# Flamingo block on one core: preparing the first feed-forward's blocks in program order, with the bias part by part and the weight combining later

## The chip, the core and the metric

The kernel runs on one core of one Trainium2 chip. The metric is the device time of one execution in microseconds (us). Before the change three runs took 2104.38, 2107.78 and 2108.16 us; the median, 2107.78 us, is the time to compare with. One more execution was profiled: it took 2106.83 us, and its trace spans 2104.7 us from the first instruction to the last.

## What is computed

Eight sequences of 512 tokens with 512 features pass through two layers, each an attention and a feed-forward, all in float32, each behind a layer norm and added back through a gate. Cut to what matters:

```python
x = x + tanh(g_xattn[0]) * linear_cross_attention(layernorm(x), ctx)
x = x + tanh(g_ffn[0])   * (gelu(layernorm(x) @ proj1.T + b1) @ proj2.T + b2)    # 512 -> 2048 -> 512
x = x + tanh(g_xattn[1]) * masked_cross_attention(layernorm(x), ctx)
x = x + tanh(g_ffn[1])   * routed_experts(layernorm(x))                          # 8 groups, silu(gate) * up, down
```

The change is in the second of these lines, the *first feed-forward* (`ff0` in the code). The weights of the fourth line (`ff1`) are combined while `ff0` runs, and the change moves that work too.

## The kernel before

**Stages.** Sequence by sequence ("block" b = 0 to 7) the kernel does the first attention (`xa0`), then all eight blocks of `ff0`, then for each block the second attention with the second feed-forward (`ff1`). Between the stages x is kept in DRAM (`between`, line 137).

**Products by fewer multiplications.** Every large matrix product is done on 2 x 2 blocks with seven products in place of eight (a Strassen-like scheme). The seven are numbered 1 to 7; some operands are sums and differences that VectorE (DVE) makes first. In `ff0` a block has four *up units* (i = 0 to 3, class `Ff0Up`, line 838) and one *down* (512 outputs). An up unit does its products in the order 1, 2, 6, 5, 7, 4, 3 (`ORDER`, line 740), of which the last two are held back until the next unit has begun (`steps`, line 1192). Its products give four quarters a11, a12, a21, a22 of the activations (`part`, line 839: DVE adds, ScalarE (ACT) applies the gelu), and `combine_inner` (line 825: three DVE instructions) makes s1 = a21 + a22, s2 = s1 - a11 and a21 = a11 - a21 of them. It is called after part (1, 2), which product 3, the last of the unit, completes.

**The split down.** From block `ONCE` = 2 on the down is a `SplitDown` (line 928): each of its seven products is again done by seven inner ones, 56 matmul instructions in a product. Its order is `SPLIT_ORDER["ff0"]` = (1, 4, 2, 6, 5, 7, 3) (line 283), the last again held back into the next block. Product 1 reads a11, 4 reads a22, 2 reads a12, 6 reads s2. For each product `combine` (line 962) makes four sums on DVE (lines 969 to 972) in tiles named `split` (seven buffers); `at_once` (line 1009) copies the result out of the PSUM accumulator (ACT, lines 1011 and 1012) and queues eight DVE instructions that join the seven inner results and add them into x (lines 998 to 1007). The accumulator has five banks, handed out in turn (`acc_bank`, line 114). So the passage from the up units to the down, here called the *handover*, reads in TensorE's (PE) order: ... products 2, 6, 5, 7 of up unit 3, down 1, up 4 and 3 of unit 3, down 4, down 2, down 6, ...

**Preparing the next block** is a generator, `prep_ff0(b)` (line 576), advanced by the main loop (lines 1485 to 1497) at evenly spaced steps of the block before, `steps_of` (line 1436) = 5 times. `normed` (line 426) takes the statistics of the four 128-token parts (DVE, lines 435 to 440), the reciprocal root on GpSimd (POOL, line 442), and then, part by part, normalizes (`norm`, line 451, DVE) and turns (`turn`, line 458 PE, 461 ACT copy). For b > 0 the statistics and the first part come in one step. After the fourth part, `prep_ff0` adds the gated bias to all four parts at once (line 581, POOL), and at the end makes the four sums S (lines 570 to 573).

**The building of weights.** For each set of weights POOL makes three or four combinations (`combining`, line 233, lines 236 to 242); for a stream used by a split down four larger ones follow (lines 412 to 419). `build_weights` and `build_stream` (lines 355, 392) load raw weights (SyncE's queue, SP), yield once, combine in two calls, and store the results by DMA. They share one buffer (`build`, line 1420). The stream of `ff0` is built during blocks 0 and 1 (every second up step), the weights of `ff1` after that, one call for every third up step (line 1477): six sets for the up units, then three for the down.

**What sets the order.** A scheduler places the instructions of an engine; only an engine named in the set `in_order` keeps the program's order (class `Ordered`, line 47). In the feed-forward stages only SP's queue is kept (line 1414). SP also carries all weight loads, into a ring of 16 tiles (`RING`, line 130), each waiting until PE has done with the tile 16 places before. So the place of another DMA in SP's order sets when it is issued.

Of the kernel before, what the change touches and what calls it, by code (L numbers as in the profile page):

```python
# [33 lines left out]
NT = S // P  # L34
# [34 lines left out]
def flamingo_kernel(  # L69
# [23 lines left out]
    in_order = {"tensor", "vector", "scalar", "gpsimd", "sync"}  # L93
# [15 lines left out]
    def psum(name):  # L109
        return bank["ps"].tile([P, 512], F32, tag="ps", name=name)  # L110
# [25 lines left out]
    xs = {}  # L136
# [96 lines left out]
    def combining(eng, w):  # L233

        sub = ALU.subtract
        eng.tensor_tensor(w[5], w[3], w[1], sub)
        yield
        eng.tensor_tensor(w[1], w[1], w[0], sub)
        yield
        eng.tensor_tensor(w[4], w[3], w[1], sub)  # L240
        yield
        eng.tensor_tensor(w[6], w[2], w[4], sub)
        yield
# [36 lines left out]

    SPLIT_ORDER = {"ff0": (1, 4, 2, 6, 5, 7, 3), "ff1": (2, 4, 1, 6, 5, 7, 3)}
    SPLIT_CHUNKS = {"ff0": NF // 4, "ff1": NJ // 4}
    SPLIT_INNER = (1, 2, 4, 5, 6, 7, 3)
    SPLIT_SLOT = {1: 0, 6: 1, 2: 2, 3: 3, 4: 4, 5: 5, 7: 6}
# [68 lines left out]
    def build_weights(ph, tile7):  # L355

        todo = {
            "ff0": (("up", raw_p1, 4), ("down", raw_p2, 4)),
            "ff1": (("up", raw_gu, 6),),
        }[ph]  # L360
        todo = [(kind, raw, i) for kind, raw, n in todo for i in range(n)]

        def load(kind, raw, i):
            t = tile7(f"{ph}_{kind}{i}")
            raw(t, i)
            return t

        if ph == "ff1":
            for kind, raw, i in todo:
                t = load(kind, raw, i)  # L370
                yield
                yield from in_twos(combining(nc.gpsimd, t))
                for q in range(7):
                    nc.sync.dma_start(out=store[ph, kind, i, q], in_=t[q])
                yield
            return
        t = load(*todo[0])
        yield
        for n, (kind, raw, i) in enumerate(todo):
            following = load(*todo[n + 1]) if n + 1 < len(todo) else None  # L380
            yield from combining(nc.gpsimd, t)
            for q in range(7):
                nc.sync.dma_start(out=store[ph, kind, i, q], in_=t[q])
            yield
            t = following

    def in_twos(steps):
        for n, _ in enumerate(steps):
            if n % 2:
                yield  # L390

    def build_stream(ph, raw, tile7):

        place = [SPLIT_ORDER[ph].index(m) for m in (1, 5, 2, 3, 6, 7, 4)]
        for i in range(SPLIT_CHUNKS[ph]):
            t = tile7(f"{ph}_down{i}")
            w = [t[:, k] for k in place]
            raw(w, i)
            yield
            yield from in_twos(combining(nc.gpsimd, w))  # L400

            b = t.rearrange("p k n (h q) -> p k n h q", q=P)
            b11, b12, b21, b22 = (b[:, :, n, h] for n in range(2) for h in range(2))

            def keep(m, w):
                nc.sync.dma_start(out=stream[ph][:, :, SPLIT_INNER.index(m), i, :], in_=w)

            sub = ALU.subtract
            for m, w in ((1, b11), (2, b21), (3, b22)):
                keep(m, w)  # L410
            yield
            nc.gpsimd.tensor_tensor(b12, b12, b11, sub)
            keep(5, b12)
            yield
            nc.gpsimd.tensor_tensor(b22, b22, b12, sub)
            keep(6, b22)
            yield
            nc.gpsimd.tensor_tensor(b21, b21, b22, sub)
            nc.gpsimd.tensor_tensor(b11, b22, b11, sub)
            keep(4, b21)  # L420
            keep(7, b11)
            yield
        streamed.add(ph)


    def normed(ph, b, tag):

        xb = xs[ph, b]
        xnT = work.tile([P, NC, S], F32, tag="xnT", name=f"xnT_{tag}")
        mv = small.tile([P, NT, 2], F32, tag="mv", name=f"mv_{tag}")  # L430
        if ph == "xa0":
            in_order.add("vector")
        for t in range(NT):
            st = small.tile([P, 6], F32, tag="st", name=f"st_{tag}_{t}")
            nc.vector.bn_stats(st, xb[:, t, :])
            nc.vector.bn_aggr(mv[:, t, :], st)
        if b:
            in_order.discard("vector")
        var = small.tile([P, NT], F32, tag="var", name=f"var_{tag}")
        nc.vector.tensor_scalar(var, mv[:, :, 1], LN_EPS, None, ALU.add)  # L440
        rstd = small.tile([P, NT], F32, tag="rstd", name=f"rstd_{tag}")
        nc.gpsimd.tensor_tensor(rstd, var, neg_half, ALU.pow)
        if ph == "xa0" or tag.startswith("ff1") or tag == "ff0_0":
            yield
        if tag.startswith("ff1"):
            yield
        xn = {}

        def norm(t):
            xn[t] = work.tile([P, D], F32, tag="xn", name=f"xn_{tag}_{t}")  # L450
            nc.vector.tensor_scalar(  # L451
                xn[t], xb[:, t, :], mv[:, t, 0:1], rstd[:, t : t + 1], ALU.subtract, ALU.mult
            )

        def turn(t):
            pt = psum(f"pt_{tag}_{t}").rearrange("p (c q) -> p c q", q=P)
            for c in range(NC):
                nc.tensor.transpose(pt[:, c, :], xn[t][:, ts(c, P)], ident)  # L458

            at = t % 2 * 2 + t // 2 if tag.startswith("ff1") else t  # L460
            nc.scalar.copy(xnT[:, :, ts(at, P)], pt)

        if ph == "xa0" and b == 0:
            norm(0)
            norm(1)
            yield
            for t in range(NT):
                turn(t)
                if t + 2 < NT:
                    norm(t + 2)  # L470
                yield
            return xnT
        for t in range(NT):
            norm(t)
            turn(t)
            yield
        return xnT

# [86 lines left out]
    def token_combinations(ph, b, xnT):  # L565

        s = work.tile([P, 4, 2, H2], F32, tag="S", name=f"S_{ph}_{b}", bufs=1)
        a11, a12 = xnT[:, 0:2, 0:H2], xnT[:, 2:4, 0:H2]
        a21, a22 = xnT[:, 0:2, H2:S], xnT[:, 2:4, H2:S]
        nc.vector.tensor_tensor(s[:, 0], a21, a22, ALU.add)  # L570
        nc.vector.tensor_tensor(s[:, 1], s[:, 0], a11, ALU.subtract)
        nc.vector.tensor_tensor(s[:, 2], a11, a21, ALU.subtract)
        nc.vector.tensor_tensor(s[:, 3], a12, s[:, 1], ALU.subtract)
        return s

    def prep_ff0(b):
        xnT = yield from normed("ff0", b, f"ff0_{b}")

        xb = xs["ff0", b]
        for t in range(NT):  # L580
            nc.gpsimd.tensor_tensor(xb[:, t, :], xb[:, t, :], b2_sb, ALU.add)  # L581
        yield "last"
        blocks["ff0", b] = xnT, token_combinations("ff0", b, xnT)

# [183 lines left out]
    class Up(Unit):  # L768
# [50 lines left out]
        def rest(self, part):  # L819
            for _ in part:  # L820
                pass
# [12 lines left out]
    def open_inner(ph, b, n):  # L834
        for k in INNER:
            inner[k] = hpool.tile([P, n, H2], F32, tag=k, name=f"{k}_{ph}_{b}")

    class Ff0Up(Up):
        def part(self, r, c, p, s):
            if (r, c) == (1, 1) and self.i == 0:  # L840
                open_inner("ff0", self.b, NF // 2)
            h = inner[f"a{r}{c}"][:, ts(self.i, 2), :]
            if s is not None:
                nc.vector.tensor_tensor(h, p, s, ALU.add)  # L844
                p = h
            yield
            for n in range(2):
                f = NF // 2 * (c - 1) + 2 * self.i + n
                nc.scalar.activation(h[:, n, :], p[:, n, :], AF.Gelu, bias=b1_sb[:, f : f + 1])  # L849
            if (r, c) == (1, 2):  # L850
                combine_inner(ts(self.i, 2))


# [74 lines left out]
    class SplitDown(Unit):  # L928
# [9 lines left out]
        def __init__(self, ph, b):  # L938
            self.ph, self.b, self.tag, self.banks = ph, b, f"{ph}_{b}_down", {}
            self.chunks, self.order = SPLIT_CHUNKS[ph], SPLIT_ORDER[ph]  # L940
            self.combined, self.numbers = {}, {}
# [132 lines left out]
    class QUp(Up):  # L1074
        ph, i = "xa0", 0
# [195 lines left out]
    ticks = iter(range(10**6))  # L1271
# [162 lines left out]
    ticks = 0  # L1434

    def steps_of(ph, b, _):

        return 5 if ph == "ff0" else 24

    at, held = None, False  # L1440
    for u, m, n in plan:
# [30 lines left out]
        if u.kind == "up":  # L1472
            ticks += 1
            if "ff0" not in streamed:
                if ticks % 2 == 0:
                    next(again, None)
            elif ticks % 3 == 0:
                next(builder, None)
        if n + 1 == 3 * B:
            continue  # L1480
# [64 lines left out]
```

## Time and profile before

| what | us |
|---|---|
| median of three runs | 2107.78 |
| profiled execution, its own time | 2106.83 |
| its span, first to last instruction | 2104.7 |
| PE busy in the span | 2061.6 (98%) |
| DVE busy | 1451.9 (69%) |
| ACT busy | 596.6 (28%) |
| POOL busy | 318.0 (15%) |

How to read it: the page gives for each engine the time in which it had an instruction under way. A matmul's record lasts longer than its pitch (one of 128 x 256 is recorded at 380 ns, and a product of eight such takes 1.73 us in the chain of work), so PE counts as busy while it merely keeps up, and only gaps larger than that show as idle. The views used below are the busy time of each engine in chosen stretches, the waits, the timeline of an engine, and the chain of work that ended last. In PE's timeline product 1 of the split down starts at 644.75 us in block 2, and at 1135.64 us in block 7, the last block of `ff0`.

### The profile page before, as it was taken

Reading aid. Unit: us, or ns where it says so; the run is one execution under the profiler, and the core shown is the slowest. Engines: PE = TensorE matmul, PEld = TensorE weight load, DVE = VectorE, ACT = ScalarE, POOL = GpSimd, SP = SyncE. Lnnn points to the kernel's source line nnn. Section 1 sums busy time; section 2 is a strip of 40 time slices with the busy share of each in tenths; the row PEclk is TensorE's granted clock in tenths of the full one; section 3 lists DMA queues with packets and bytes.
Section 4 is the critical chain, followed back from the end, with each engine's and each line's share of the span. In section 5 each row is a group of like instructions: output and inputs, shape, how many; then the busy total and the mean of one; then the engine's idle time right before and its main releaser. Section 6 shows DMA issues by size and latency. Waiting matters only on the chain.

```text
span 2104.7 us, 34195 instructions
## 1 busy us (share of the span) xinstructions
PE 2061.6 (98%) x12460; PEld 1816.1 (86%) x12460; DVE 1451.9 (69%) x2727; ACT 596.6 (28%) x1236; POOL 318.0 (15%) x260
## 2 busy tenths in 40 slices
PE   8999999999999999999999999999999999999998
PEld 4778887788889998889898989898989889898988
DVE  3688777652528494868667777777777677876768
ACT  3433333222222324132334232213222222222121
POOL 3122111342413112240301010000000010100000
PEclk9999999999999999999999999999999999999999
DMA  7345633696869898888875858686776858585865
GB/s 227 120 155 155 209 132 93 214 306 220 294 220 330 285 307 288 283 298 281 297 248 190 304 163 276 198 264 214 229 237 189 283 170 293 157 284 161 269 204 169
DMA packets 306501, 485.12 MB, mean 230 GB/s; under 512 B 37024, under 2 KB 107840, under 8 KB 302240
## 3 DMA queue, kind: packets, MB, share of 16 engines
q1 hardware_dynamic: 298896, 456.18, 67.7%
q10 hardware_dynamic: 5856, 23.20, 2.9%
q0 software_dynamic: 1584, 3.57, 0.7%
q8 instruction: 100, 1.64, 0.3%
q14 instruction: 65, 0.53, 0.1%
HBM read 406.22 MB, written 76.61 MB: 229 GB/s over the span
## 4 chain that ended last, share of the span: by engine, by line
PE 74%; issue 10%; DVE 7%; DMA 4%; POOL 3%; SPq 1%; ACT 1%; ACTq 0%; POOLq 0%; DVEq 0%
PE x_ff L789 23%; PE w_ff L789 11%; PE x_ff_down L984 9%; PE w_ff_down L984 7%; PE z_ff L789 6%; PE z_ff_down L984 3%; PE v_ff_down L984 3%; PE x_ff_down L905 2%; SPq L60 1%; PE w_ff_down L905 1%; PE pt_ff L458 1%; PE pt_xa L458 1%; PE pst L609 1%; PE pr L654 1%; PE z_ff_down L905 1%
## 5 line engine op out<-in xcount | busy, mean ns | idle before, releaser
L789 PE MATMUL x_ff<-S_ff,w_ff_up 128*128 128x256 f32 x1280 | 304.5, 381 | 1.7 <-ACT u_ff L801 1.7
L789 PE MATMUL w_ff<-S_ff,w_ff_up 128*128 128x256 f32 x1280 | 303.6, 380 | 1.5 <-DVE a_ff L844 1.5
L789 PE MATMUL x_ff<-xnT_ff,w_ff_up 128*128 128x256 f32 x1280 | 294.1, 380 | 0.9 <-ACT u_ff L801 0.9
L801 ACT COPY u_ff<-x_ff 128x512 f32<-128x512 f32 x240 | 139.5, 582 | 539.2 <-PE x_ff L789 520.3
L789 PEld LDWEIGHTS x_ff<-S_ff,w_ff_up 128*128 128x128 f32 x1280 | 239.9, 190 | 42.6 <-issue 6.5
L789 PEld LDWEIGHTS w_ff<-S_ff,w_ff_up 128*128 128x128 f32 x1280 | 239.0, 190 | 34.2 <-DVE a_ff L844 2.3
L789 PEld LDWEIGHTS x_ff<-xnT_ff,w_ff_up 128*128 128x128 f32 x1280 | 238.4, 190 | 32.9 <-ACT u_ff L801 1.8
L789 PE MATMUL z_ff<-xnT_ff,w_ff_up 128*128 128x256 f32 x640 | 151.6, 379 | 0.0
L984 PE MATMUL x_ff_down<-w_ff_down,split_ff_down 128*128 128x128 f32 x1152 | 136.4, 275 | 2.8 <-DVE split_ff_down L972 1.9
L984 PEld LDWEIGHTS x_ff_down<-w_ff_down,split_ff_down 128*128 128x128 f32 x1152 | 132.2, 192 | 3.6 <-DVE split_ff_down L972 2.2
L789 PEld LDWEIGHTS z_ff<-xnT_ff,w_ff_up 128*128 128x128 f32 x640 | 119.8, 190 | 15.3
L849 ACT ACTIVATE a_ff<-a_ff,b_sb 128x256 f32<-128x256 f32 x128 | 58.1, 501 | 155.1 <-DVE a_ff L844 155.0
L984 PE MATMUL w_ff_down<-w_ff_down,split_ff_down 128*128 128x128 f32 x768 | 90.8, 275 | 1.1 <-DVE split_ff_down L972 1.1
L828 DVE TENSOR_TENSOR s_ff<-a_ff,a_ff 128x512 f32<-128x512 f32 x56 | 45.8, 819 | 65.4 <-ACT a_ff L849 65.4
L984 PEld LDWEIGHTS w_ff_down<-w_ff_down,split_ff_down 128*128 128x128 f32 x768 | 88.2, 192 | 1.3 <-DVE split_ff_down L972 1.3
L998 DVE TENSOR_TENSOR part_ff_down<-part_ff_down 128x128 f32<-128x128 f32 x245 | 72.6, 313 | 23.4 <-ACT part_ff_down L1011 17.5
L844 DVE TENSOR_TENSOR a_ff<-w_ff,u_ff 128x512 f32<-128x512 f32 x64 | 43.8, 684 | 60.1 <-ACT u_ff L801 60.1
L872 DVE SCALAR_TENSOR_TENSOR g_ff<-th_ff,x_ff 128x512 f32<-128x512 f32 x48 | 32.9, 685 | 70.4 <-ACT th_ff L871 70.4
L882 DVE TENSOR_TENSOR up_ff<-w_ff,u_ff 128x512 f32<-128x512 f32 x96 | 65.6, 683 | 17.7 <-ACT u_ff L801 17.7
L581 POOL TENSOR_TENSOR x_ff<-x_ff,b_sb 128x512 f32<-128x512 f32 x28 | 39.3, 1408 | 253.5 <-DVE xn_ff L451 253.5
L451 DVE TENSOR_SCALAR xn_ff<-x_ff,mv_ff,rstd_ff 128x512 f32<-128x512 f32 x64 | 41.2, 661 | 48.2 <-PE pt_ff L458 36.4
L984 PE MATMUL w_ff_down<-w_ff_down,s_ff 128*128 128x128 f32 x576 | 70.2, 275 | 0.0
(274 smaller groups left out, 3665.2 us busy)
## 6 DMA issues: line engine op xcount, KB each, us to landing
w_ff_down<-stream_ff SPq DMA_DIRECT2D x582, 256.0 KB
w_ff_up<-ff_up SPq DMA_DIRECT2D x560, 256.0 KB
stream_ff<-build_ff_down SPq DMA_DIRECT2D x49, 448.0 KB
x_ff<-x_ff SPq DMA_DIRECT2D x16, 1024.0 KB
share<-shares SPq DMA_DIRECT2D x64, 256.0 KB
w_ff_down<-ff_down SPq DMA_DIRECT2D x56, 256.0 KB
ff_up<-build_ff_up SPq DMA_DIRECT2D x42, 256.0 KB
spread<-over SPq DMA_DIRECT2D x32, 256.0 KB
```

The lines of the kernel that those rows point to most:

```text
L451: nc.vector.tensor_scalar(xn[t], xb[:, t, :], mv[:, t, 0:1], rstd[:, t : t + 1], ALU.subtract, ALU.mult)
L458: nc.tensor.transpose(pt[:, c, :], xn[t][:, ts(c, P)], ident)
L581: nc.gpsimd.tensor_tensor(xb[:, t, :], xb[:, t, :], b2_sb, ALU.add)
L789: nc.tensor.matmul(p[:, n, :], lhsT=w[:, c, ts(n, P)], rhs=moving, **self.mark(m, 2 * n + c),)
L801: nc.scalar.copy(self.s[m], p)
L828: nc.vector.tensor_tensor(s1, a21, a22, ALU.add)
L844: nc.vector.tensor_tensor(h, p, s, ALU.add)
L849: nc.scalar.activation(h[:, n, :], p[:, n, :], AF.Gelu, bias=b1_sb[:, f : f + 1])
L882: nc.vector.tensor_tensor(u, p, s, ALU.add)
L905: nc.tensor.matmul(p[:, t, :], lhsT=a[:, k, ts(t, P)], rhs=w[k // 2][:, k % 2, :], **self.mark(m, 2 * k + t),)
L984: nc.tensor.matmul(p[bank][:, place, :], lhsT=operand[k][:, c, :], rhs=w[at // 4][:, ts(at % 4, P)], start=bank not in opened, stop=True, ...
L998: return lambda: nc.vector.tensor_tensor(m(k), m(k), m(by), ALU.add)
```

## The change

Five things change, all in `ff0` or in the building beside it:

1. `normed` for `ff0` and b > 1 keeps DVE's statistics and normalizations in program order, yields after the reciprocal root, then does `norm(0)` alone in a step, and from then on normalizes part t + 1 in the step that turns part t. The steps of a preparation go from 5 to 7.
2. The bias of a part is added by POOL right after that part is turned, for all blocks of `ff0`.
3. The order of the split down becomes 1, 4, 6, 2, 5, 7, 3.
4. `combine_inner` of an up unit is called after part (2, 1), product 4, in place of part (1, 2), product 3.
5. The building of the `ff1` weights waits four calls, not one, between loading a set and combining it, and is called at every second up step, not every third.

```diff
-    SPLIT_ORDER = {"ff0": (1, 4, 2, 6, 5, 7, 3), "ff1": (2, 4, 1, 6, 5, 7, 3)}
+    SPLIT_ORDER = {"ff0": (1, 4, 6, 2, 5, 7, 3), "ff1": (2, 4, 1, 6, 5, 7, 3)}
...
                 t = load(kind, raw, i)
-                yield
+                for _ in range(4):
+                    yield
                 yield from in_twos(combining(nc.gpsimd, t))
...
             raw(w, i)
-            yield
+            for _ in range(1 if ph == "ff0" else 4):
+                yield
             yield from in_twos(combining(nc.gpsimd, w))
...
-    def normed(ph, b, tag):
+    def normed(ph, b, tag, normed_part=lambda t: None):
...
-        if ph == "xa0":
+        ordered = ph == "ff0" and b > 1
+        if ph == "xa0" or ordered:
             in_order.add("vector")
...
-        if ph == "xa0" or tag.startswith("ff1") or tag == "ff0_0":
+        if ph in ("xa0", "ff0") or tag.startswith("ff1"):
             yield
...
             xn[t] = work.tile([P, D], F32, tag="xn", name=f"xn_{tag}_{t}")
+            if ordered:
+                in_order.add("vector")
             nc.vector.tensor_scalar(
                 xn[t], xb[:, t, :], mv[:, t, 0:1], rstd[:, t : t + 1], ALU.subtract, ALU.mult
             )
+            if ordered:
+                in_order.discard("vector")
...
+        if ordered:
+            norm(0)
+            yield
         for t in range(NT):
-            norm(t)
+            if not ordered:
+                norm(t)
+            elif t + 1 < NT:
+                norm(t + 1)
             turn(t)
+            normed_part(t)
             yield
         return xnT
...
     def prep_ff0(b):
-        xnT = yield from normed("ff0", b, f"ff0_{b}")
-
         xb = xs["ff0", b]
-        for t in range(NT):
+
+        def biased(t):
+
             nc.gpsimd.tensor_tensor(xb[:, t, :], xb[:, t, :], b2_sb, ALU.add)
+
+        xnT = yield from normed("ff0", b, f"ff0_{b}", biased)
         yield "last"
...
-            if (r, c) == (1, 2):
+            if (r, c) == (2, 1):
                 combine_inner(ts(self.i, 2))
...
-        return 5 if ph == "ff0" else 24
+        return 7 if ph == "ff0" else 24
...
-            elif ticks % 3 == 0:
+            elif ticks % 2 == 0:
                 next(builder, None)
```

## The prediction

> **What bounds the kernel now.** I read the page first: its busy times, then the shares of the chain that ended last.
>
> ```profile
> PE 2061.6 (98%) x12460; PEld 1816.1 (86%) x12460; DVE 1451.9 (69%) x2727; ACT 596.6 (28%) x1236; POOL 318.0 (15%) x260
> ```
> ```profile
> PE 74%; issue 10%; DVE 7%; DMA 4%; POOL 3%; SPq 1%; ACT 1%; ACTq 0%; POOLq 0%; DVEq 0%
> ```
>
> PE sets the end. The diff leaves its matmul count alone, so only its stalls and its clock can change. Next I took the period from one block's product 1 to the next in PE's timeline. Product 1 starts at 644.75 (block 2), 740.83, 834.86, 936.28, 1033.91 and 1135.64 us (block 7); the periods are 96.08, 94.03, 101.42, 97.63 and 101.73. The last holds extra matmuls of the second feed-forward's preparation and stays. Block 3's 94.03 is undisturbed. Blocks 2, 4 and 5 exceed it by 2.05, 7.39 and 3.60: **13.04 us, or 0.62%, is the ceiling of any gain here**.
>
> Then I read busy time by stretch. Columns: stretch, its length, busy us (instructions) of PE, PEld, DVE, ACT and POOL, granted clock, DMA share, GB/s.
>
> ```profile
> 665.00:690.00 25.00, 23.33 (x200) 22.74 (x199) 24.24 (x48) 3.97 (x9) 5.85 (x4) 1.00 0.93 323
> 716.00:741.00 25.00, 25.00 (x122) 22.04 (x121) 11.78 (x23) 11.26 (x24) 6.61 (x6) 1.00 0.96 321
> 741.00:759.00 18.00, 18.00 (x148) 17.59 (x148) 17.30 (x24) 5.05 (x11) 8.81 (x6) 1.00 0.95 318
> 759.00:784.00 25.00, 25.00 (x218) 24.79 (x217) 24.24 (x55) 3.94 (x9) 0.00 (x0) 1.00 0.90 300
> 835.00:857.00 22.00, 18.20 (x138) 17.41 (x137) 20.70 (x30) 5.05 (x11) 12.56 (x8) 0.95 0.82 283
> 884.00:910.00 26.00, 25.07 (x145) 22.45 (x144) 15.33 (x25) 8.73 (x19) 7.80 (x5) 1.00 0.95 316
> 936.00:957.00 21.00, 19.02 (x149) 17.98 (x148) 19.85 (x28) 4.94 (x11) 11.85 (x6) 1.00 0.93 306
> ```
>
> DVE is 47% busy in an up phase (11.78 of 25), 96% in block 3's handover (17.30 of 18), 97% in its down (24.24 of 25). PE loses time where POOL works beside a full DVE: 3.80 us in block 4's handover (22.00 - 18.20), 1.98 in block 5's, 1.67 in block 2's down. Block 4's handover by DVE's timeline, then POOL's:
>
> ```profile
> 838.55 0.68 DVE L844 TENSOR_TENSOR a_ff<-w_ff,u_ff 128x512 f32<-128x512 f32 x1
> 839.15 0.17 DVE L436 BATCH_NORM_AGGREGATE mv_ff<-st_ff 128x2 f32<-128x6 f32 x1
> 839.36 0.44 DVE L440 TENSOR_SCALAR var_ff<-mv_ff 128x4 f32<-128x4 f32 x1
> 840.93 1.49 DVE L451 TENSOR_SCALAR xn_ff<-x_ff,mv_ff,rstd_ff 128x512 f32<-128x512 f32 x1 [1.13 <-POOL rstd_ff L442]
> 842.34 1.75 DVE L969 TENSOR_TENSOR split_ff_down<-a_ff 128x512 f32<-128x512 f32 x1
> 848.77 2.56 DVE L972 TENSOR_TENSOR split_ff_down<-a_ff,split_ff_down 128x512 f32<-128x512 f32 x1
> ```
> ```profile
> 838.04 1.73 POOL L236 TENSOR_TENSOR build_ff_down<-build_ff_down 128x512 f32<-128x512 f32 x1 [17.91 <-DMA build_ff_down<-in_dn]
> 843.50 1.72 POOL L581 TENSOR_TENSOR x_ff<-x_ff,b_sb 128x512 f32<-128x512 f32 x1
> 848.26 2.52 POOL L412 TENSOR_TENSOR build_ff_down<-build_ff_down 128x896 f32<-128x896 f32 x1
> ```
>
> DVE prepares the next block between two splits, waits 1.13 us for POOL's root, and its instructions stretch from 0.68 to 1.75 or 2.56 us. The chain of waits puts the price on product 2:
>
> ```profile
> 855.04 7.99 PE z_ff_down L984 x56
> 863.03 6.25 PE x_ff_down L984 x56
> ```
>
> It starts after a 2.5 us wait for its last a12 (the longest of PE's waits) and runs at a lower granted clock, 7.99 for 6.25 us: 1.74 more.
>
> [...]
>
> **The change, part by part.** T0 is the start of a block's product 1.
>
> *Statistics and norms.* In calm stretches a statistic takes 0.675 us, its aggregate 0.175, the variance 0.17, a norm 0.547. A handover of blocks 2 to 5 loses 4 x 0.675 + 4 x 0.175 + 0.17 + 2 x 0.547 = **4.66 us of DVE**, and the wait for the root. In the built order they now stand in the up phase of the same block: statistics and norm 0 in unit 0, the rest in units 1 and 2. That cover is half empty (11.78 us in 25), so I cost them at nothing there; uncovered they would cost 4.66 us a block. Block 6's handover alone keeps its statistics, for the second attention. The new wait for the root stands in DVE's kept order, with additions of unit 0 behind it, on which PE waits. The root takes 1.02 us and a step of the preparation is about 7 us, so nothing shows unless POOL stands before an unlanded set: from 0 to a few us; I take 0.
>
> *Turnings.* Same number; PE's and ACT's instructions move within the up phase. 0.
>
> *Bias.* Same four POOL additions of 1.26 to 1.73 us, out of the handover into the up phase. They took part in stretching block 4's splits. Beside a DVE with half its time free: 0.
>
> *Split order and combine_inner.* The sum of the handover's DVE work is unchanged. Product 2 gets another product, 6.25 us, of time before its a12 is due; product 6 needs s2 instead. Its path is a22, part 1's eight joins, s1, a12, s2, split 6: by calm durations s2 is ready 12.5 us after T0 and the third sum of split 6 at 16.0, as product 6 starts (15.95) and 5.36 us before that sum is due. Product 2's last sum is ready at 23.4 and due at 27.6: **4.2 us of slack** where before 2.5 us were missing. What is late next is product 6's split, if POOL stretches it. The fifth product in the new order also takes the accumulator bank that product 2 has just closed. ACT's copy of 0.58 us stands against 0.89 us (eight matmuls) of grace; the old order had the same reuse one place earlier and no such wait. 0 to 1.5 us over all blocks; I take 0.3.
>
> *Building, later and more often.* Loads and stores are SP's: the ring of weights runs 16 tiles ahead, a down eats one in 0.89 us and an up unit one in 1.73, so even a blocked SP of about 6 us (block 5, where the second down set's load waits for the first set's stores) leaves ten tiles. No wait of PE on weights shows before; I take 0. Combining moves by four calls at two steps each. From the positions in SP's built order and a load latency of 10.8 us (first issue 827.2, POOL starts 838.04), the up sets land either in up phases or from T0 - 1 to T0 + 5, before the splits that matter. Down set 0 comes in block 5's up (eight operations out of block 4's handover). Down set 1's first five come about T0 + 12 to T0 + 21 in block 5's down. Down set 2's last three (2.2 to 2.5 us each) come about T0 + 17 to T0 + 25 in block 6's. There DVE is 97% busy: this is the price. Block 5: a stretch of 4 x 1.07 (1.75 - 0.68) + 1.9 (2.56 - 0.68) = 6.2 us against 4.2 of slack, at least 0 and at most 6.2; I take 1.0. Block 6: 3 x 1.9 = 5.7, at least 0 and at most 5.7; I take 1.8.
>
> **Sum.** Ceiling 13.04. It leaves: small stalls of up phases with combining in them, 1.84 now (884 to 910: 0.93; 910 to 936: 0.27; 1008 to 1034: 0.64), plus 0.5; block 5's down 1.0; block 6's down 1.8; banks 0.3; other 0.6. Together 6.0, so the gain is **7.0 us**. Against the profiled execution's own 2106.83 that is 2099.8. The median of the runs lies 0.95 above it: **2100.8 us**.
>
> **The rivals.** *The full ceiling* (0.25): POOL's work in the downs stretches only instructions with slack. Gain 10.4 to 13.0, 2094.8 to 2097.4, about 2096. For it: block 4's 12.56 us of POOL cost 5.5 us of PE, but with 4.66 us of DVE work and an ordered wait that are now gone. Against it: in block 2's down 5.85 us of POOL alone cost 1.67.
>
> *The contention only moves* (0.22): POOL's sums fall into the two downs with a stretch of 11.9 us, and most of it ends on PE, with one half-clock product. Gain or loss within 4.2 us, about 2105 to 2107. It covers the case that the change does no more than shift a stall.
>
> *Slower* (0.08): the same mechanism, at its worst place. If DVE in the downs of blocks 5 and 6 has no slack at all, because the late splits already trail PE when POOL starts, all 6.2 + 5.7 = 11.9 us become stalls, with two half-clock products at 1.74 (3.5). With the 1.84 and 0.5 of the up phases, 0.3 and 0.6, that leaves 18.6 us where the ceiling returns 13.04: +5.6, some 2113 us. It ends slower from the point where more than 13.04 - 3.2 = 9.8 us of stretch and clock loss reach PE in these two downs. Against it: in block 3's down, without POOL, DVE at 97% costs PE nothing, so it is not behind when POOL starts.
>
> **How the numbers follow.** Likeliest case, 0.45: gain 4.2 to 10.4, 2097.4 to 2103.6, at 2100.8. A measurement of this kernel can tell about 0.2%, 4.2 us; its three runs spread over 3.8. Faster by more: 0.45 + 0.25 = 0.70; within: 0.22; slower: 0.08. The range 2094.5 to 2106.5 takes in the ceiling and most of the moved contention.
>
> **What would show it.** Right: in blocks 2 to 5 no statistic or norm between split 1 and split 6; splits at 0.68 us in block 4's handover; no 7.99 us product; periods of blocks 2 and 4 near 94 and 95. Block 5's and 6's downs show POOL's 2.2 to 2.5 us sums beside stretched splits, with PE waits of 1 to 2 us. Wrong: a wait for a root with up additions behind it; PE waiting on weights in block 5; product 5 or 7 waiting for ACT's copy; or a 1.74 us clock loss in a down, which alone would take a quarter of the gain.

## The result: slower by a quarter of a per cent

| | before | after |
|---|---|---|
| median of 12 runs, us | 2106.76 | 2111.63 |
| lowest and highest, us | 2102.68, 2108.94 | 2103.65, 2116.74 |
| ratio, with its 95% interval | 1 | 1.0026 [1.0014, 1.0038] |
| span of the profiled execution, us | 2104.7 | 2111.0 |

The forecast was 2100.8 us. The change makes the kernel slower by about 5 us. Lines of the changed kernel lie about 16 further down: L844 to L846 are the three additions of `combine_inner` (L828 to L830 before), L860 is the add that empties an accumulator (L844), L985 to L988 are the splits (L969 to L972), L1000 the matmul of the split down (L984), L817 ACT's copy out of the accumulator (L801). The page and the chain:

```profile
PE 2065.3 (98%) x12460; PEld 1816.6 (86%) x12460; DVE 1449.2 (69%) x2727; ACT 595.4 (28%) x1236; POOL 323.1 (15%) x260
...
PE 77%; DVE 8%; issue 8%; DMA 3%; ACT 2%; POOL 1%; SPq 1%; ACTq 0%; DVEq 0%; POOLq 0%
```

The shares hardly move, except that ACT, 1% of the chain before, has 2%. A view that tells the stages apart is needed. First the handover, which the change was argued on. Busy time by stretch (columns as in the prediction): block 4's handover, block 2's down, and block 5's handover.

```profile
843.00:865.00 22.00, 22.00 (x185) 21.59 (x184) 20.82 (x35) 5.07 (x11) 3.33 (x3) 1.00 0.94 321
674.00:699.00 25.00, 25.00 (x219) 24.79 (x218) 21.99 (x55) 4.45 (x9) 0.00 (x0) 1.00 0.88 290
939.00:960.00 21.00, 21.00 (x173) 20.53 (x172) 18.47 (x33) 5.17 (x11) 9.46 (x2) 1.00 0.71 233
```

PE is busy throughout: the 3.80, 1.67 and 1.98 us that these places lost before are back. The chain of waits has block 4's product 6 and then product 2, both at 6.25 us, where before the granted clock fell to 0.50 in product 2 (856 to 858 us of its trace):

```profile
858.75 6.25 PE x_ff_down L1000 x56
865.01 6.25 PE z_ff_down L1000 x56
```

So the handover did what was forecast. Now PE's waits in blocks 0 and 1, which the prediction had not looked at (us in total, times, longest):

```profile
PE x_ff L805 <- ACT u_ff L817: 5.2, 4, 2.1
PE pt_ff L465 <- DVE xn_ff L60: 1.5, 1, 1.5
PE z_ff_down L921 <- ACT a_ff L865: 0.5, 1, 0.5
```

Before, the same view had two waits, 1.2 and 0.8. The loss by place, from the starts of product 1 in PE's timeline ("up 0" is from the first matmul of `ff0` to block 0's product 1, "b2" from block 2's product 1 to block 3's), with the runs that follow:

| us | up 0 | b0 | b1 | b2 | b3 | b4 | b5 | b6 |
|---|---|---|---|---|---|---|---|---|
| before | 44.90 | 100.94 | 98.45 | 96.08 | 94.03 | 101.42 | 97.63 | 101.73 |
| after | 49.02 | 106.00 | 98.45 | 94.30 | 94.24 | 96.80 | 99.74 | 102.93 |
| e1_combine_late | 44.90 | 98.45 | 98.45 | 93.88 | 93.88 | 94.16 | 97.58 | 109.08 |
| e3_before_combine_early | 48.59 | 103.11 | 99.13 | 96.44 | 94.72 | 100.11 | 97.96 | 101.73 |
| e6_before_prep | 44.90 | 98.45 | 98.45 | 93.88 | 93.88 | 96.69 | 94.22 | 101.73 |
| e7_before_building | 44.90 | 100.99 | 98.45 | 96.48 | 96.01 | 96.64 | 98.95 | 108.99 |
| e8_later_sets | 44.91 | 98.45 | 98.45 | 93.88 | 93.88 | 93.88 | 94.03 | 102.13 |

After minus before: +4.12 and +5.06 at the head, then 0, -1.78, +0.21, -4.62, +2.11, +1.20; together +6.3, the difference of the two spans. Blocks 2 and 4 gain as forecast (94.30 and 96.80 us, where some 94 and 95 were expected); the up units of blocks 0 and 1, where nothing was expected, and the down between them take 9.2. (The idle time that a view gives is some 0.16 us less than what a stall costs from start to start, since a matmul is recorded that much longer than its pitch: 0.38 us for 1.73 / 8. The recorded expectations count from start to start, the text below as the views do.)

What happens there, in block 0's first up unit. DVE, POOL, ACT and PE, each from its timeline:

```profile
413.79 2.05 DVE L844 TENSOR_TENSOR s_ff<-a_ff,a_ff 128x512 f32<-128x512 f32 x1 [3.01 <-ACT a_ff L865]
415.87 1.64 DVE L845 TENSOR_TENSOR s_ff<-s_ff,a_ff 128x512 f32<-128x512 f32 x1
417.44 1.75 DVE L846 TENSOR_TENSOR a_ff<-a_ff,a_ff 128x512 f32<-128x512 f32 x1
419.11 0.68 DVE L860 TENSOR_TENSOR a_ff<-w_ff,u_ff 128x512 f32<-128x512 f32 x1
```
```profile
414.00 1.28 POOL L238 TENSOR_TENSOR build_ff_down<-build_ff_down 128x512 f32<-128x512 f32 x1
415.36 1.61 POOL L240 TENSOR_TENSOR build_ff_down<-build_ff_down 128x512 f32<-128x512 f32 x1
417.05 1.59 POOL L242 TENSOR_TENSOR build_ff_down<-build_ff_down 128x512 f32<-128x512 f32 x1
```
```profile
419.82 0.91 ACT L865 ACTIVATE a_ff<-a_ff,b_sb 128x256 f32<-128x256 f32 x2 [6.07 <-DVE a_ff L860]
420.64 0.56 ACT L817 COPY u_ff<-x_ff 128x512 f32<-128x512 f32 x1
```
```profile
421.25 1.99 PE L805 MATMUL x_ff<-S_ff,w_ff_up 128*128 128x256 f32 x8 [1.47 <-ACT u_ff L817]
```

And the same place in the kernel before, DVE's timeline:

```profile
415.13 1.78 DVE L829 TENSOR_TENSOR s_ff<-s_ff,a_ff 128x512 f32<-128x512 f32 x1
416.84 0.68 DVE L844 TENSOR_TENSOR a_ff<-w_ff,u_ff 128x512 f32<-128x512 f32 x1
417.44 1.16 DVE L830 TENSOR_TENSOR a_ff<-a_ff,a_ff 128x512 f32<-128x512 f32 x1
```

The reader is to follow one chain. `combine_inner` is now called before product 3's part, so its three additions, with both inputs in SBUF, stand in DVE's queue ahead of the add that product 3 needs (L860). POOL reads SBUF beside them, and they take 2.05, 1.64 and 1.75 us where 0.69 is usual. The add comes at 419.11 instead of 416.84. ACT sits idle for 6.07 us before the gelu of that part; the copy that empties an accumulator bank (L817) stands behind the gelu and starts at 420.64, though the product that it copies had ended at 418.06, and PE waits for it, 1.47 us. Before, the add stood between the second and the third addition.

### The profile page after: what moved, and what is told of

Read it like the earlier page. It is cut to its first block, busy times and chain, and to the rows that moved or that the text cites. A ratio compares the mean times of both kernels' runs of the same rounds, so it can differ in the third digit from the quotient of the medians.

```text
span 2111.0 us, 34196 instructions
## 1 busy us (share of the span) xinstructions
PE 2065.3 (98%) x12460; PEld 1816.6 (86%) x12460; DVE 1449.2 (69%) x2727; ACT 595.4 (28%) x1236; POOL 323.1 (15%) x260
## 3 DMA queue, kind: packets, MB, share of 16 engines
q8 instruction: 100, 1.64, 0.3%
## 4 chain that ended last, share of the span: by engine, by line
PE 77%; DVE 8%; issue 8%; DMA 3%; ACT 2%; POOL 1%; SPq 1%; ACTq 0%; DVEq 0%; POOLq 0%
PE x_ff L805 25%; PE w_ff L805 11%; PE x_ff_down L1000 10%; PE w_ff_down L1000 7%; PE z_ff L805 6%; PE v_ff_down L1000 3%; PE z_ff_down L1000 3%; PE x_ff_down L921 3%; PE w_ff_down L921 1%; PE pt_ff L465 1%; DVE s_ff L845 1%; SPq L60 1%; PE pt_xa L465 1%; DVE a_ff L846 1%; DVE s_ff L844 1%
## 5 line engine op out<-in xcount | busy, mean ns | idle before, releaser
L817 ACT COPY u_ff<-x_ff 128x512 f32<-128x512 f32 x240 | 139.6, 583 | 534.4 <-PE x_ff L805 515.5
L1000 PE MATMUL x_ff_down<-w_ff_down,split_ff_down 128*128 128x128 f32 x1152 | 135.6, 275 | 0.6 <-DVE split_ff_down L985 0.6
L1000 PEld LDWEIGHTS x_ff_down<-w_ff_down,split_ff_down 128*128 128x128 f32 x1152 | 132.0, 192 | 0.8 <-DVE split_ff_down L985 0.8
L860 DVE TENSOR_TENSOR a_ff<-w_ff,u_ff 128x512 f32<-128x512 f32 x64 | 43.9, 685 | 86.8 <-ACT u_ff L817 86.8
L844 DVE TENSOR_TENSOR s_ff<-a_ff,a_ff 128x512 f32<-128x512 f32 x56 | 46.8, 836 | 67.8 <-ACT a_ff L865 67.8
L445 POOL TENSOR_TENSOR rstd_ff<-var_ff,neg_half 128x4 f32<-128x4 f32 x15 | 15.3, 1023 | 495.1 <-DVE var_ff L443 442.1
L1000 PE MATMUL w_ff_down<-w_ff_down,split_ff_down 128*128 128x128 f32 x768 | 90.3, 275 | 0.0
L1000 PEld LDWEIGHTS w_ff_down<-w_ff_down,split_ff_down 128*128 128x128 f32 x768 | 88.0, 192 | 0.0
L1000 PE MATMUL w_ff_down<-w_ff_down,s_ff 128*128 128x128 f32 x576 | 70.2, 275 | 0.0
L1000 PE MATMUL x_ff_down<-w_ff_down,a_ff 128*128 128x128 f32 x576 | 69.0, 275 | 0.0
```

What stands on the lines that cost most here:

```text
L817: nc.scalar.copy(self.s[m], p)
L844: nc.vector.tensor_tensor(s1, a21, a22, ALU.add)
L1000: nc.tensor.matmul(p[bank][:, place, :], lhsT=operand[k][:, c, :], rhs=w[at // 4][:, ts(at % 4, P)], start=bank not in opened, stop=True, ...
```

## The experiments

Theory P (placement) is this chain. Rival N says that the norms, bias additions and denser building, which now lie in the up phases, cost there wherever `combine_inner` stands. The first four runs tell them apart. Line numbers are each run's own and shift by a few; the names of the tiles tell what a line is.

**e1_combine_late**, one part undone:

```diff
-            if (r, c) == (2, 1):
+            if (r, c) == (1, 2):
                 combine_inner(ts(self.i, 2))
```

> The changed kernel with one part undone: combine_inner is called after part (1, 2), product 3, again. Theory P (placement): the changed kernel is slow because combine_inner, called one product earlier in all 32 up units, puts three additions with both inputs in SBUF ahead of the add that empties product 3's accumulator, and POOL's combining stretches them, so ACT's copy and PE come late. Blocks 0 and 1 then give back their 9.1 us (product 1 of block 2 starts at about 645 us, not 654.1), the up phases of blocks 4 to 6 some 3.9 (stalls of 5.7 back to about 1.8): 2098 us, 2095 to 2101. Rival N: the norms, the bias additions and the denser building now stand in the up phases, and cost there wherever combine_inner stands: 2111, within 2. The prediction's own step said that product 6 needs the early s2; if so, PE waits for split 6 in every block from 2 on, up to 2 us each.

Measured: 2098.51 us, 0.9964 [0.9950, 0.9977] of before. P holds: up 0 is 44.90 again, b0 98.45. No product 6 waits for s2 from its late combining; with the preparation out of the handover that supposed need isn't there (with it, in e5 below, product 6 does wait). What P did not name is b5 and b6, taken up below.

**e2_combine_last_unit**, early only where the new order could use it:

```diff
-            if (r, c) == (2, 1):
+            if (r, c) == ((2, 1) if self.i == 3 and self.b >= ONCE else (1, 2)):
```

> The changed kernel, with combine_inner after part (2, 1) only in up unit 3 of blocks 2 to 7, where the split down needs s2 early, and after part (1, 2) in all other units. P: 2098 us, as with all of it undone or up to 2 us better if s2 was late there; block 2's product 1 at about 645 us. What stays is the 2.22 us stall ahead of block 5's down (935 us), which lies in unit 3. N: 2111, within 2.

Measured: 2098.35 us, 0.9965 [0.9953, 0.9978]. As the run before, so the early sums bring nothing that can be measured even in unit 3. The 2.22 us stall that was expected to stay is gone too: the expectation had its unit wrong. The additions ahead of it are unit 2's, whose last two products run after unit 3's first, and for unit 2 this run combines late. POOL's large sums are still there (915.18 to 920.24 us), but the add stands ahead of the third addition again:

```profile
918.21 0.68 DVE L860 TENSOR_TENSOR a_ff<-w_ff,u_ff 128x512 f32<-128x512 f32 x1
918.81 1.98 DVE L846 TENSOR_TENSOR a_ff<-a_ff,a_ff 128x512 f32<-128x512 f32 x1
```

**e3_before_combine_early**, that part alone on the kernel before:

```diff
-            if (r, c) == (1, 2):
+            if (r, c) == (2, 1):
```

> The kernel before with one part of the change alone: combine_inner after part (2, 1). P: blocks 0 and 1 are as in the changed kernel and lose 9 us, the up phases of blocks 4 to 6 with combining beside them 1 to 4 more: 2116 to 2120 us. N: no change, 2107 within 2.

Measured: 2113.89 us, 1.0037 [1.0025, 1.0049]: some 8 us, a little under the 9 to 13 expected. N predicted no change and falls. PE's waits in its blocks 0 and 1:

```profile
PE x_ff L789 <- ACT u_ff L801: 5.8, 4, 2.1
PE z_ff_down L905 <- ACT a_ff L849: 1.7, 2, 1.2
```

**e4_clearing**, the changed kernel with its order kept, but POOL's subtractions replaced by memsets of their outputs (the combined weights are left out):

```diff
+    def clearing(w):
+        for k in (5, 1, 4, 6):
+            nc.gpsimd.memset(w[k], 0.0)
+            yield
...
-                yield from in_twos(combining(nc.gpsimd, t))
+                yield from in_twos(clearing(t))
...
-            nc.gpsimd.tensor_tensor(b12, b12, b11, sub)
+            nc.gpsimd.memset(b12, 0.0)
```

> The changed kernel with POOL's combining of the first feed-forward's down weights and of all second feed-forward weights left out: each subtraction is replaced by a memset of its output, so POOL writes SBUF at the same places but doesn't read it. P[...]: combine_inner's instructions take 0.69 us each in all up units, the stalls of the up phases (14.1 us of single waits and some 3 of half-clock products) nearly vanish, and the downs of blocks 5 and 6 lose their 0.9 and 1.1: 2092 to 2096 us. If the order alone makes PE wait, or the bias additions do (N), it stays above 2105.

Measured: 2093.18 us, 0.9939 [0.9924, 0.9955]. Without the sums of POOL's building the order does no harm: PE is busy for all 13.00 us from 411 to 424, where the changed kernel has 11.53. DVE's second and third addition (L845 and L846 of the changed kernel) and POOL's memset in block 0:

```profile
412.79 0.69 DVE L850 TENSOR_TENSOR s_ff<-s_ff,a_ff 128x512 f32<-128x512 f32 x1
413.39 0.68 DVE L851 TENSOR_TENSOR a_ff<-a_ff,a_ff 128x512 f32<-128x512 f32 x1
```
```profile
413.16 0.84 POOL L419 MEMSET build_ff_down<- 128x896 f32 x1 [2.07 <-DMA build_ff_down<-in_p]
```

A memset of 128 x 896, which only writes SBUF, lies across both additions, and they stay at 0.69 and 0.68; beside POOL's sums, which read it too, the same two take 1.64 and 1.75 us in the changed kernel. That the reading makes the difference is an estimate from these two cases. (The memsets are also shorter, 0.84 for 2.1 us, so part of the gain is that less overlaps.) Late combining with POOL's sums beside it (e1) and early combining without them (e4) both leave up 0 at 44.9: the stall needs both.

The next four take the other parts one by one, and try to mend what e1 and e2 left.

**e5_before_order**, the split order alone:

```diff
-    SPLIT_ORDER = {"ff0": (1, 4, 2, 6, 5, 7, 3), ...
+    SPLIT_ORDER = {"ff0": (1, 4, 6, 2, 5, 7, 3), ...
```

> The kernel before with the new split order (1, 4, 6, 2, 5, 7, 3) alone; combine_inner stays after part (1, 2). The prediction's step: product 2's late a12 cost 2.66 and 0.57 us of waiting in blocks 4 and 5 and 1.74 of half clock, and goes; what is late next is split 6. Theory O (order is a main part of the gain): 2101 to 2103 us. Rival: with DVE as full as before the wait only moves from product 2 to product 6's splits: 2105 to 2107, with PE waiting for split sums of product 6 in blocks 4 and 5.

Measured: 2105.00 us, 0.9990 [0.9982, 0.9999]. The rival is nearer. In block 4 the wait has moved from product 2's a12 to product 6's s2:

```profile
PE x_ff_down L984 <- DVE s_ff L829: 2.4, 1, 2.4
PE v_ff_down L984 <- DVE split_ff_down L972: 1.3, 1, 1.3
```

**e6_before_prep**, the preparation alone (items 1 and 2 of the change, with its seven steps):

> The kernel before with the preparation alone: seven steps, statistics and norms kept in program order, bias part by part; split order, combine_inner and building as before. Theory D (the 4.66 us of DVE work and the ordered wait for the root, which leave the handovers, are the main part): blocks 4's and 5's handovers keep POOL's combining but little else; gain 4 to 6 us, 2100 to 2102. Rival: the stretch of the splits by POOL's combining is what costs, and stays: 2104 to 2106. If instead the norms in the up phase cost PE time there, waits for L860's counterpart show in blocks 2 to 6.

Measured: 2093.90 us, 0.9944 [0.9930, 0.9959]: 12 to 13 us, more than twice theory D's forecast. b0 gives 2.5, b2 2.2, b4 4.7, b5 3.4. POOL's combining still stands in block 4's handover, and PE loses nothing by it:

```profile
829.00:851.00 22.00, 22.00 (x184) 21.59 (x184) 20.37 (x29) 5.04 (x11) 8.29 (x5) 1.00 0.96 333
```

POOL is busy for 8.29 us beside DVE; before it was 12.56, with the root and two bias additions, which moved out with the norms. So the combining alone costs nothing here. That it had no part in the loss of before doesn't follow; e7, next, shows that it had. What stays in b4 are two waits in block 5's up phase, 1.35 and 0.93 us. The second is for an add that stands in DVE's order right behind the four statistics, 3.4 us of work with their aggregates and the variance, so their new place isn't quite free.

**e7_before_building**, the building alone:

```diff
-                yield
+                for _ in range(4):
+                    yield
...
-            elif ticks % 3 == 0:
+            elif ticks % 2 == 0:
```

> The kernel before with the building alone: four calls between load and combining, a call at every second up step. Theory D: the stretch only moves, from block 4's handover to the downs of blocks 5 and 6, where DVE is as full: 2104 to 2108 us. Rival B (POOL's combining in block 4's handover is the main cost, about 5.5 us): 2100 to 2102.

Measured: 2112.07 us, 1.0027 [1.0015, 1.0038], slower than both theories said. b4 gains 4.8, but b3 loses 2.0, b5 1.3 and b6 7.3. Busy time in block 4's handover:

```profile
837.00:859.00 22.00, 20.09 (x163) 19.44 (x163) 20.32 (x36) 4.99 (x11) 8.58 (x7) 1.00 0.91 317
```

The statistics, the norms and DVE's wait for the root are all still in it, while POOL is busy for 8.58 us, not 12.56. PE loses 1.91 us, for product 2's late a12, where before it lost 3.80 and 1.74 by a lower clock; with as much of POOL and without the preparation (e6) it loses nothing. The stall of before was the two together. Blocks 2 and 3 now have a wait for a12 too, 1.71 and 1.87 us: sets combined more often fall into their handovers.

In b6 PE waits 2.85 us for a split in the handover and 0.85 and 1.14 in the down, and the clock is 0.91 over the 19 us of the handover (1.7 us). The longest wait isn't POOL's doing. SP's timeline, then DVE's and PE's:

```profile
1020.33 5.88 SPq L60 DMA_DIRECT2D build_ff_down<-in_dn  x10
1027.73 0.38 SPq L60 DMA_DIRECT2D x_ff<-x_ff  x1
```
```profile
1035.79 1.29 DVE L437 BATCH_NORM_STATS2 st_xa<-x_ff 128x6 f32<-128x512 f32 x2 [7.68 <-DMA x_ff<-x_ff]
1037.80 0.67 DVE L971 TENSOR_TENSOR split_ff_down<-a_ff 128x512 f32<-128x512 f32 x1
```
```profile
1038.53 3.83 PE L986 MATMUL x_ff_down<-w_ff_down,split_ff_down 128*128 128x128 f32 x18 [2.85 <-DVE split_ff_down L971]
```

SP issues the x of the second attention's preparation behind ten loads of the last down set, 5.1 us ahead of product 1, where the kernel before does it 12.2 us ahead. The statistics of that x stand in DVE's order before product 1's splits, and DVE sits idle for 7.68 us. Only the waits in the down are the prediction's price for POOL beside full DVE work. The plainest view of that price is in e1_combine_late, whose b6 is 7.35 over: in block 6's down DVE's timeline, POOL's, and busy time by stretch.

```profile
1043.56 2.57 DVE L986 TENSOR_TENSOR split_ff_down<-split_ff_down,a_ff 128x512 f32<-128x512 f32 x1
1046.06 2.57 DVE L987 TENSOR_TENSOR split_ff_down<-a_ff 128x512 f32<-128x512 f32 x1
1048.55 2.49 DVE L1014 TENSOR_TENSOR part_ff_down<-part_ff_down 128x128 f32<-128x128 f32 x2
1050.96 2.28 DVE L1048 TENSOR_TENSOR s_ff<-a_ff,s_ff 128x2048 f32<-128x2048 f32 x1
1053.16 0.68 DVE L988 TENSOR_TENSOR split_ff_down<-a_ff,split_ff_down 128x512 f32<-128x512 f32 x1
```
```profile
1041.16 4.43 POOL L417 TENSOR_TENSOR build_ff_down<-build_ff_down 128x896 f32<-128x896 f32 x1 [11.56 <-DMA stream_ff<-build_ff_down]
1045.66 2.41 POOL L420 TENSOR_TENSOR build_ff_down<-build_ff_down 128x896 f32<-128x896 f32 x1
1048.04 2.53 POOL L421 TENSOR_TENSOR build_ff_down<-build_ff_down 128x896 f32<-128x896 f32 x1
```
```profile
1041.00:1053.00 12.00, 9.73 (x88) 9.54 (x86) 11.97 (x11) 0.97 (x2) 9.33 (x3) 0.99 1.03 374
1053.00:1066.00 13.00, 12.10 (x84) 12.10 (x85) 12.62 (x33) 1.93 (x4) 0.00 (x0) 0.74 0.58 179
```

Three POOL sums stretch three DVE instructions (the one of 128 x 2048 takes its usual 2.28 us); product 2's last split comes at 1053.16, and PE waits 3.2 us in the middle of the product. Then the granted clock is 0.74 for 13 us, which costs as much again (13 x 0.26 = 3.4). Elsewhere shorter waits were followed by a lower clock too (last section).

**e8_later_sets**, e2 with two loads put off, so that the combining of the last two down sets falls into no handover or down:

```diff
             w = [t[:, k] for k in place]
+            if ph == "ff1" and i:
+                for _ in range(3 * i - 1):
+                    yield
             raw(w, i)
```

> The changed kernel with combine_inner early in unit 3 of blocks 2 to 7 only, and the loads of the second and third down set of the second feed-forward put off by two and five calls, so that none of them is issued while POOL or SP is still at the set before, and no combining falls into a handover or a down. In the kernel without the delay PE waits 1.21 + 0.47 us in block 5 (SP issues the second set's twelve loads in 8.9 us just at product 1, and weights come late) and 0.81 + 3.34 in block 6 (POOL's combining beside the handover and the down). If these causes are right, both go: periods of blocks 5 and 6 at 93.9, 2098.35 - 5.8 = 2092.5 us, 2091 to 2095. If the combining, now in block 7's up phase beside the second feed-forward's preparation, costs there what it saves: 2096 to 2099.

Measured: 2089.53 us, 0.9924 [0.9910, 0.9939], better than forecast because b6 gave back the clock loss too. (Its period is 102.13, not the 93.9 expected: it holds extra matmuls of the second feed-forward's preparation, as before, when it was 101.73.) Its two stretches of block 6, handover and down:

```profile
1016.00:1038.00 22.00, 22.00 (x184) 21.59 (x183) 20.14 (x41) 5.18 (x11) 1.02 (x1) 1.00 0.81 255
1038.00:1063.00 25.00, 25.00 (x219) 24.80 (x218) 20.65 (x57) 4.46 (x9) 0.00 (x0) 1.00 0.89 286
```

PE is full and every block from 2 to 5 takes 93.88 to 94.03: this part of the kernel has no stall left to take. The cause named for block 5 shows in the traces too. In e2, SP's timeline had the load of the second set just before PE needs weights, and PE's waits over its `ff0` blocks named that stream:

```profile
926.44 8.93 SPq L60 DMA_DIRECT2D build_ff_down<-in_dn  x12
```
```profile
PE v_ff_down L1000 <- DMA w_ff_down<-stream_ff: 1.0, 1, 1.0
```

The twelve loads occupy SP just when PE leaves the up units and needs seven weight tiles for each 6.25 us. In e4, which leaves the combining out, PE waits for the same stream, 1.1 and 0.7 us, so this isn't POOL's doing. In e1 the same place waits 2.6 us; its view names a DVE sum of the next preparation, which that product doesn't read, while SP had issued the next weights only at 938.08 us, 3.1 us before PE went on.

The last four ask which part of the preparation brings its 12 us, and whether the new order is needed at all.

**e9_prep_unordered**, e6 without keeping the order (the seven steps and the bias part by part stay):

```diff
-        if ph == "xa0" or ordered:
+        if ph == "xa0":
             in_order.add("vector")
...
-            if ordered:
-                in_order.add("vector")
```

> The kernel before with the new preparation, seven steps and bias part by part, but without keeping DVE's statistics and norms in program order. In the built order the statistics of the block after next then stand in the handover again, with the wait for the root. Theory D (the gain of the preparation alone, 12 to 13 us, comes from DVE's order): only block 1's part of it is left, 2.5 us, so 2103 to 2106. Rival (the finer steps or the bias part by part bring it): 2094.

Measured: 2104.75 us, 0.9993 [0.9983, 1.0002]. The gain is gone, and DVE's timeline of block 4's handover is that of the kernel before:

```profile
835.49 0.17 DVE L437 BATCH_NORM_AGGREGATE mv_ff<-st_ff 128x2 f32<-128x6 f32 x1
835.70 0.43 DVE L441 TENSOR_SCALAR var_ff<-mv_ff 128x4 f32<-128x4 f32 x1
837.26 1.49 DVE L452 TENSOR_SCALAR xn_ff<-x_ff,mv_ff,rstd_ff 128x512 f32<-128x512 f32 x1 [1.13 <-POOL rstd_ff L443]
838.67 1.75 DVE L979 TENSOR_TENSOR split_ff_down<-a_ff 128x512 f32<-128x512 f32 x1
```

The scheduler had hoisted the statistics from a later preparation; here only the kept order pulls them out.

**e10_prep_bias_last**, e6 with the four bias additions at the end again:

```diff
-        xnT = yield from normed("ff0", b, f"ff0_{b}", biased)
+        xnT = yield from normed("ff0", b, f"ff0_{b}")
+        for t in range(NT):
+            biased(t)
```

> The kernel before with the new preparation, in program order, but all four bias additions after the last turning, as before. D: 2094 us, within 1.5, as with the bias part by part: the additions only need to be out of the way of DVE's splits, and the built order leaves DVE's instructions alone. Rival: the bias additions, four in a row (5 to 7 us of POOL) near the handover, stretch the splits: 2097 to 2100.

Measured: 2093.11 us, 0.9932 [0.9919, 0.9945], like e6. The bias part by part is worth nothing here.

**e11_before_block1_yield**, one line of the kernel before:

```diff
-        if ph == "xa0" or tag.startswith("ff1") or tag == "ff0_0":
+        if ph == "xa0" or tag.startswith("ff1") or tag in ("ff0_0", "ff0_1"):
```

> The kernel before with one line changed: block 1's preparation yields after the reciprocal root, so that its first norm no longer stands right behind the root on DVE. In all kernels with the new preparation block 0 takes 98.45 us from product to product, in the kernel before and those without it 100.9 to 103.4, with PE waiting 1.3 to 2.6 us for an addition of unit 0. If that norm's wait for POOL is the cause: 2104.5 us (2.5 less), block 0 at 98.45. If it is noise of the building in block 0: no change, 2107.

Measured: 2106.45 us, 0.9997 [0.9989, 1.0006], and b0 still at 100.66. A miss. DVE in block 0's down still waits 1.15 us for a root, but that line can't help it: in the built order these statistics are block 2's, hoisted two blocks ahead, and e6, whose kept order begins with block 2, has none in this place. Keeping the order is what frees b0 fully; part of the gain comes without it, since e9 has b0 at 99.35.

**e12_later_sets_old_order**, e8 with the old split order and combining after part (1, 2):

> The kernel with the down sets' loads put off (2089.5 us), with the old split order (1, 4, 2, 6, 5, 7, 3) and combine_inner after part (1, 2) in all units. If the new split order and the early combining are not needed once the handover is free of the preparation and of POOL's combining: 2089.5, within 1, periods of blocks 2 to 6 at 93.9 to 94.1. If product 2's a12 is still late in the old order (4.66 us less work against 2.5 us missing leaves 2.1 us of slack): some 0 to 1.5 us in each of five blocks, 2092 to 2096.

Measured: 2092.02 us, 0.9924 [0.9911, 0.9937], the same ratio as e8's (each is against the kernel before on its own chip). In the trace b5 is 94.95 for 94.03, with one wait of 0.81 us in block 5's down. So between nothing and about a microsecond is left for the new order.

## Why the prediction was wrong

**The step that failed** is "Split order and combine_inner. The sum of the handover's DVE work is unchanged." The edit was costed in the handover alone, where `combine_inner` feeds product 6. But it stands in `Ff0Up.part`, which all 32 up units run; only the six last units of blocks 2 to 7 stand ahead of a split down. In the other 26 the early call has nothing to give, and what is queued behind the three additions on DVE, the add of product 3, was not asked for. The prediction had asked just that of the wait for the root. From the table, after minus e1 is 4.12 and 7.55 in up 0 and b0, 0.4 each in b2 and b3, 2.6 and 2.2 in b4 and b5: **17.3 us** in these places, where the prediction had 0. Some 3.5 of it is a lower clock in block 1's up units (0.86 over 25 us), after two such waits. (In b6 after is 6.2 better than e1, so the two differ by 11 us of span, and by 13 in the medians. The three sums began 18 us after block 6's product 1 in after and 19 in e1, but the first took 2.19 us in one and 4.43 in the other. Why they mesh differently isn't settled.) Alone on the kernel before, the early call costs 8 us. The cost could have been bounded from rows of before: its trace has L828 to L830 at up to 2.2 and 2.5 us beside POOL, so an early call could put some 3 us of stretch ahead of an add in every unit with combining beside it. The range, which stopped at 2106.5, should have held that.

**The ceiling** of 13.04 us measured blocks 2, 4 and 5 against block 3 and left block 0 out. It missed 2.5 in b0, where block 2's hoisted statistics made PE wait. By e8's periods it is 2.49 + 2.20 + 0.15 + 7.54 + 3.60 (b0, b2 to b5): 16.0.

**Statistics and norms:** right, and undersized. Their move brings 12 to 13 us alone and clears the handovers and downs of blocks 2 to 5; in block 5's up units PE's waits, 0.93 and 0.27 us before, are 1.35 and 0.93 in e6, where nothing was expected. "PE loses time where POOL works beside a full DVE" was read too simply: the prediction's own row 741 to 759 has POOL at 8.81 us and DVE at 96%, and PE loses nothing. By e6 and e7 block 4's stall needed the preparation and POOL's work together.

**Bias, turnings and the wait for the root:** costed at 0, and so measured alone (e6, e10; no wait of PE behind a root shows in the up phases). In the changed kernel one turning did wait 1.5 us, for a norm that stands in DVE's order behind the stretched additions (block 1).

**Split order:** the slack of product 2 was right, but the gain was the preparation's already; alone the order only moves the wait to s2 (e5), and after the preparation it brings at most about 1 us (e12).

**Building:** its direction was right, its size not. The two downs were put at 1.0 and 1.8. The runs have 7.3 in block 6 twice: in e1 3.2 of it is a wait in the down and 3.4 a lower clock; in e7 2.85 is the late load of x, 2.0 waits in the down and 1.7 a lower clock. In the changed kernel there are only single waits of 0.69 and 0.93 in the downs. Loads, taken at 0 because SP is blocked for about 6 us, cost that 2.85 in e7, 1.3 us in block 5 in e2 and, as argued above, 2.6 in e1: the 6 to 9 us in which SP issues ten or twelve loads were left out, though each was in the built order.

**The rivals.** The slower rival's 2113 us lies next to the measured 2111.63, but that is chance: its place, the downs of blocks 5 and 6, cost under 2 us in the changed kernel. That the other terms sum up to e1's -7.6 (0.9964), against the forecast of -7.0, is no proof of them either: a ceiling too low and downs too cheap made up for each other.

## What to carry to other kernels

Cost an edit to a shared helper at every place that calls it, and at each ask what stands behind it in its engine's queue; here the harm was in 26 units that the edit wasn't made for. DVE additions placed ahead of the instruction that empties an accumulator were cheap here only where POOL made no sums beside them: three of 0.69 us became 5.4, and ACT and PE followed. Measure the parts apart: here one part was worth some -12 us, one +5 and one +8, and their sum hid that the first alone beats both kernels by 12 us or more; with the building changed and its loads put off (e12) it is 16.

## What the runs showed of the hardware

- Where POOL's sums ran beside DVE's work, both took longer. A 128 x 512 addition of DVE goes from 0.68 to 2.57 us beside POOL's sums, a norm from 0.55 to 2.29 (changed kernel, block 1), and a POOL sum of 128 x 896 from 2.08 to 4.43 us; even a DVE join of 128 x 128, 0.28 us, takes 2.17 us beside a POOL sum (e1, block 6). The adds of the changed kernel that read one input from the accumulator (L860) did not stretch: all 93 took 0.67 to 0.69 us, that of 419.11 us in the middle of a POOL sum (418.72 to 421.13).
- A wait of 3.2 us was followed by 13 us at a granted clock of 0.74, as dear as the wait (e1, block 6). In the changed kernel one of 1.97 us in block 6's up units was followed by a lower clock too (0.83 over the 10 us from 1020 us, 0.51 in 1024 to 1026); one of 2.12 us in block 0's up units and one of 2.06 us ahead of block 5's down left it at 1.00 (424 to 449 and 937 to 950 us). So the length of a wait alone doesn't settle it, and what does is not shown here. In block 1 of the changed kernel it was lower after waits of 1.47 and 1.41 us, 2 us apart (0.50 in 526 to 529 us):

```profile
520.00:545.00 25.00, 22.12 (x94) 18.48 (x93) 9.90 (x14) 10.68 (x23) 12.40 (x7) 0.86 0.86 260
```

- SP took 8.93 us (e2) to issue twelve loads of the second feed-forward's down weights, 0.74 us each, one after another, and 7.8 to 8.4 in e4, the changed kernel and e1; a queue's order must be costed in issue time and not only in what it waits for.
